# Two layers of attention and routed experts on one core: the queue that the maxima's rows are sent on, and when and how many blank rows are laid

## The chip, the cores and the metric

The kernel runs on one core of a Trainium2 chip. The time is what the device takes for one execution, in microseconds (us). It was measured in nine runs before the change, with a median of 740.36 us (735.84 to 743.92). One further execution was recorded by the hardware profiler. That one took 738.56 us, and all durations below are from it.

The core has five engines that each work through their own instructions in order: PE (TensorE, matrix products), DVE (VectorE), ACT (ScalarE), POOL (GpSimd) and SP (SyncE, which does nothing but issue transfers, load registers and wait). Transfers between DRAM and on-chip memory (DMA) are issued by SP, ACT or POOL, and carried out by 16 DMA engines. The profile names the queue of a transfer: q1 holds what SP issues, q10 what ACT issues, q0 what POOL issues.

## The reference

Four steps, each added to `x` (8 blocks of 256 tokens, 128 wide, 2048 tokens in all):

```python
x = x + _L0_xattn_ref(_layernorm(x), ctx, ctx, mask, mask, Wq, bq, Wk, bk, Wv, bv)
x = x + _L0_ffn_ref(_layernorm(x), W_router, b_router, W1, b1, W2, b2)
x = x + _L1_xattn_ref(_layernorm(x), ctx, ctx, w_q, w_k, w_v, w_o)
x = x + _L1_ffn_ref(_layernorm(x), W_gate, Wg, Wu, Wd)
```

Layer 0's attention has 16 heads of width 8, and a pair of tokens whose mask bits differ gets -1e9 added to its score before the softmax. Layer 0's feed-forward part sends each token to the two of 8 experts with the largest logits, weighted with a softmax over these two:

```python
logits = flat_x @ W_router + b_router
top_vals, top_idx = jax.lax.top_k(logits, 2)
router_weights = softmax(logits, all but the two largest at -inf)
for e in range(8):
    h = relu(flat_x @ W1[e] + b1[e])          # 128 -> 512
    y = h @ W2[e] + b2[e]                     # 512 -> 128
    out = out + y * router_weights[:, e] * (token has e among its two)
```

Layer 1 is of the same kind: causal attention with 16 heads of width 64 and an output projection, and experts of width 352 with a silu gate.

## The kernel before

**Layer 0's attention.** One step of the main loop (its counter `n`) handles a pair of heads of one tile of queries. For block `b`, `scores` computes the scores q k for 125 of 128 contraction rows and DVE takes each query's maximum (L546, L550). The softmax needs that maximum subtracted. It is subtracted by the matrix product itself: rows 125 to 127 of the query operand `q9` hold the maxima, split in three bf16 parts, and the same rows of the key operand `k9` hold -1. `probs` then computes the transposed scores anew with all 128 rows (L577), and ACT takes the exponential (L584). `probs` runs `LAG` = 15 steps behind `scores`.

The rows of maxima come from `maxima(b, hf)`, once for each half of the heads, so 16 times in all: DVE splits the maxima, PE transposes them (L565), ACT copies the result to `mT` (24 partitions of 256 bf16 values, L569), and a DMA of 12 KB sends `mT` into the three rows of `q9` (L570). SP issues that DMA. The first `probs` of the half wait for it.

SP also loads the operands of the blocks to come. In `prep0(b)`, which starts two blocks ahead, it sends four mask rows (L446), writes the three parts of q and k to DRAM in another layout (`rows<-part`, L531, six DMAs of 192 KB) and loads `q9` and `k9` from there (`q<-rows`, `k<-rows`, L534 and L535, 576 KB each). The parts are computed by POOL (L514 to L517). SP works in program order, so one of its instructions that waits holds all that come behind it.

**Routing.** `route` takes 4 (or 2) tiles of 128 tokens, finds each token's two experts and the slot in each expert's list, and POOL writes the token's normalised row there with an indirect DMA (`xs<-rows,ati`, L712: one DMA for 128 tokens and one of their two experts). `taken[l][:, k, e]` is the first free slot of expert `e` after `k` token tiles. Layer 0's first 12 of 16 token tiles (`NEARLY`) are routed while the attention runs, the last four after it.

Each expert's list is worked on in tiles of 128 rows, so rows that are no token's follow behind the last slot. They must hold a valid row address and a weight of zero, and are called blank rows. `blank` is a DRAM buffer of such rows, and `spread` copies from it into a stretch of an expert's list in `xs`. For layer 0 that is `tails(0)`: for each of the 8 experts SP loads the first free slot into a register (`values_load`) and issues a DMA there. Before the change this happens as soon as the first 12 token tiles are counted, with `taken` at tile 12, and each stretch is five tiles of 128 rows (640 rows of 520 bytes, 325 KB), so that it reaches past what the last four token tiles can add; their rows are written over it afterwards. Layer 1 lays its blank rows in another way (`blanks(1)`).

**Tables and experts.** `place(l, early)` makes the list of expert tiles. Its early call takes the 16 tiles that are full after 12 token tiles; its late call takes the other 23. `tab` holds the expert and the row of each tile. The expert loop `run` then works through the 39 tiles, four ahead with its loads: `look_up(j)` loads expert and row of tile `j` from `tab` into SP's registers, `fetch(j)` issues two DMAs, the tile's rows (`xj<-xs`, L815, 65 KB) and its expert's weights (`wj<-wa`, L822, 258 KB in layer 0 and 352 KB in layer 1), `flip` transposes the rows (`px`, L827, PE), `hidden` makes the hidden layer (`ph`, L842), and `result` the output, which POOL writes to `ys` with another indirect DMA (L882). The rows of an early tile wait only for the early scatters; those of a late tile wait for all scatters and for the blank rows.

**What sets the order.** PE, ACT, DVE and SP execute their instructions in the order in which the program text emits them. POOL's queue is left to a scheduler. Pieces of work that run beside the main loop are generators in the list `side`; each call of `tick()` advances each of them to its next `yield`. `one_by_one` puts generators behind one another in one of these. The end of the passage from attention to experts reads, in the main loop and behind it:

```python
        if n == NS * B + LAG - 2:
            begin0(range(4))
            tiles0 = run0()
        if n >= NS * B + LAG:
            next(tiles0)
    one_by_one(route(0, NT - QT, QT))
    one_by_one(place(0, False))
```

The first expert tiles are thus worked on while the last two token tiles are still being routed.

Of the kernel before, what the change touches and what calls it, by code (L numbers as in the profile page):

```python
# [17 lines left out]
P = 128  # L18
# [11 lines left out]
GT = G // P  # L30
NG = B * S // G
T = B * S
NT = T // P
# [3 lines left out]
NX = E * XT + E * P  # L37
# [4 lines left out]
NEARLY = NT - 4  # L42
EARLY = (16, 17)
FIRST = EARLY[0] + QT * E
HH = H // 2
# [8 lines left out]
R_ALL = P  # L54
R_MAX = R_ALL - NPART
# [7 lines left out]
def kernel(  # L63
# [28 lines left out]
    nc = tc.nc  # L92
# [7 lines left out]
    ET = mybir.EngineType  # L100
# [4 lines left out]
    def bank(tag, name, dt=F32):  # L105

        if tag == "any":
            third.append(third.pop(0))
            tag = third[-1]
        return ps.tile([P, 512 * 4 // mybir.dt.size(dt)], dt, tag=tag, name=name, bufs=1 if tag in ("pv", "y") else 2)  # L110

    writes = {}
    known = {}

    def after(dma, key, n=None):

        if n is not None:
            for group in (key + "late", key + "blank"):
                tc.declare_no_dep(dma.ins, group=group, reason="disjoint rows")
        tc.add_to_no_dep_group(key + "read", dma.ins)  # L120
        for w in writes.get(key, ())[:n]:
            tc.add_manual_dep(
                dma.ins, w.ins.name,
                mybir.DependencyInfo(mybir.DependencyClass.Sync, mybir.DependencyReason.DATA),
                reason="rows by index",
            )
        return dma
# [13 lines left out]
    side = []  # L141
# [46 lines left out]
    with nc.allow_non_contiguous_dma(reason="two rows of biases, once"):  # L188
        for i, src in enumerate((bq0, bk0)):
            nc.scalar.dma_start(  # L190
                out=brow[:, i, :].rearrange("o (d g j) -> o d g j", d=DK0, g=4),
                in_=src.rearrange("(o j z) g -> o z g j", o=1, z=32)[:, :DK0],
# [94 lines left out]
    q9s, k9s = [], []  # L287
# [23 lines left out]
    xs = [dr.tile([NX, ROW], F32, tag=f"xs{l}", name=f"xs{l}") for l in range(2)]  # L311
# [21 lines left out]
    taken = [cst.tile([P, NT + 1, E], F32, tag=f"tk{l}", name=f"tk{l}") for l in range(2)]  # L333
# [218 lines left out]
    def maxima(b, hf):  # L552

        mx = c0[b]["mx"][:, :, ts(hf, HH)]
        m3 = sm.tile([P, QT, NPART, HH], BF16, tag="m3", name=f"m3_{b}_{hf}")
        rest = sm.tile([P, QT, HH], F32, tag="mrest", name=f"mrest{b}_{hf}")
        nc.vector.tensor_copy(m3[:, :, 0, :], mx)
        nc.vector.tensor_tensor(rest, mx, m3[:, :, 0, :], ALU.subtract)
        nc.vector.tensor_copy(m3[:, :, 1, :], rest)
        nc.vector.tensor_tensor(m3[:, :, 2, :], rest, m3[:, :, 1, :], ALU.subtract)  # L560
        yield
        yield
        pm = bank("pt", f"pm{b}_{hf}", BF16)
        for qt in range(QT):
            nc.tensor.transpose(  # L565
                pm[: NPART * HH, ts(qt, P)], m3[:, qt].rearrange("p r h -> p (r h)"), ident_b
            )
        mT = sm.tile([NPART * HH, S], BF16, tag="mT", name=f"mT{b}_{hf}")
        nc.scalar.copy(mT, pm[: NPART * HH, :S])  # L569
        nc.sync.dma_start(out=q9s[b % 3][R_MAX:R_ALL, ts(hf, HH), :], in_=mT)  # L570
        yield

    def probs(b, h):
# [44 lines left out]
    def route(l, t0, GT, eng=nc.vector):  # L618
# [11 lines left out]
        def s8(tag):  # L630
            return sm.tile([P, GT, E], F32, tag=tag + str(GT), name=f"{tag}{name}", bufs=1)
# [48 lines left out]
        for i in range(GT):  # L680
            k = t0 + i
            eng.tensor_tensor(taken[l][:, k + 1, :], taken[l][:, k, :], pr[:, 1, i, :], ALU.add)
        if t0 + GT == NEARLY and l == 0:
            side.append(tails(l))
        rank = s8("rank")
        eng.tensor_tensor(rank, pr[:, 0], taken[l][:, tiles, :], ALU.add)
        slot = sm.tile([P, 2, GT, E], F32, tag=f"slot{GT}", name=f"slot{name}", bufs=1)
# [17 lines left out]
        for i in range(GT):  # L705
            for k in range(2):
                if eng is nc.gpsimd and (k == 0 or t0 < NEARLY - GT):
# [5 lines left out]
                        out=xs[l][:, :], out_offset=to, in_=rows[:, i, k, :], in_offset=None  # L713
# [5 lines left out]
    def place(l, early):  # L719

        n, m = (NEARLY, EARLY[l]) if early else (NT, NJ - EARLY[l])
        if early:
            known[f"xs{l}"] = len(writes[f"xs{l}"])
        name = f"{l}_{n}"
        cnt = sm.tile([P, E + 1], F32, tag="cnt", name=f"cnt{name}", bufs=1)
        nc.vector.tensor_tensor(cnt[:, :E], own, taken[l][:, n, :], ALU.mult)
        nc.vector.tensor_reduce(cnt[:, E:], cnt[:, :E], AX.X, ALU.add)
        cnt = cnt[:, E:]
        is_in = sm.tile([P, 2], F32, tag="isin", name=f"isin{name}", bufs=1)
        if early:  # L730
            nc.vector.tensor_scalar(is_in[:, 0:1], cnt, -float(P), what[:, 1:2], ALU.add, ALU.is_ge)
        else:
            nc.vector.tensor_tensor(is_in[:, 1:2], cnt, what[:, 1:2], ALU.is_gt)
            nc.vector.tensor_tensor(is_in[:, 0:1], is_in[:, 1:2], tabs[l, "taken"], ALU.subtract)
        in_b = sm.tile([P, 1], BF16, tag="inb", name=f"inb{name}", bufs=1)
        nc.vector.tensor_copy(in_b, is_in[:, 0:1])
        yield
        yield
        pos = bank("pt", f"pos{name}")[:, 0:1]
        nc.tensor.matmul(pos, lhsT=upper, rhs=in_b, start=True, stop=True)  # L740
        at = sm.tile([P, 1], F32, tag="pos", name=f"at{name}", bufs=1)
        nc.vector.tensor_copy(at, pos)
        pick = sm.tile([P, NJ], F32, tag="pick", name=f"pick{name}", bufs=1)
        nc.vector.tensor_scalar(pick[:, :m], order[:, :m], at, is_in[:, 0:1], ALU.is_equal, ALU.mult)
        if early:
            got = tabs[l, "taken"] = sm.tile([P, 1], F32, tag="got", name=f"got{name}", bufs=1)
            nc.vector.tensor_scalar(got, at, m - 0.5, is_in[:, 0:1], ALU.is_lt, ALU.mult)
        yield
        yield
        po = bank("pt", f"pick{name}")[:m, :3]  # L750
        nc.tensor.matmul(po, lhsT=pick[:, :m], rhs=what, start=True, stop=True)
        tab = sm.tile([P, 2], I32, tag=f"tab{early}", name=f"tab{name}", bufs=1)
        if early:
            nc.vector.tensor_copy(tab[:m, :], po[:, :2])
        else:
            sp = sm.tile([P, 4], F32, tag="sp", name=f"sp{name}", bufs=1)
            nc.vector.tensor_copy(sp[:m, :3], po)
            nc.vector.tensor_scalar(sp[:m, 3:4], sp[:m, 2:3], spare[:m, 1:2], spare[:m, 0:1], ALU.mult, ALU.add)
            nc.vector.tensor_copy(tab[:m, 0:1], sp[:m, 0:1])
            nc.vector.tensor_tensor(tab[:m, 1:2], sp[:m, 1:2], sp[:m, 3:4], ALU.add)  # L760
        tabs[l, early] = tab
        yield

    def spread(to, i):

        to = to.rearrange("(c a r) w -> a c (r w)", a=16, r=P // 16)
        src = blank[i, :, : P // 16 * ROW].unsqueeze(1)
        return nc.sync.dma_start(out=to, in_=src.to_broadcast(list(to.shape)))

    def tails(l):  # L770

        last = sm.tile([P, E], I32, tag="last", name=f"last{l}", bufs=1)
        nc.vector.tensor_copy(last, taken[l][:, NEARLY, :])
        m = NT - NEARLY + 1
        for i in range(E):
            if i % 2 == 0:
                yield
            row = nc.values_load(
                last[0:1, i : i + 1], engines=(ET.SP,), min_val=0, max_val=NX - m * P,
                skip_runtime_bounds_check_because="an expert has XT rows",  # L780
            )
            dma = spread(xs[l][bass.ds(row, m * P), :], i)

            for group in (f"xs{l}", f"xs{l}blank"):
                tc.declare_no_dep(dma.ins, group=group, reason="disjoint rows")
            tc.add_to_no_dep_group(f"xs{l}blank", dma.ins)
# [7 lines left out]
    def experts(l):  # L794
# [16 lines left out]
        def fetch(j):  # L811
            e, row, _ = regs[j]
            xj = wk.tile([P, ROW], F32, tag="xj", name=f"xj{l}_{j}", bufs=10)
            after(
                nc.sync.dma_start(out=xj, in_=xs[l][bass.ds(row, P), :]), f"xs{l}",  # L815
                known[f"xs{l}"] if j < EARLY[l] else None,
            )
            src = (wa0, wa1)[l]
            if j % 2 == 0:
                tiles["w"] = wk.tile([P, 2, 2 * FF1], F32, tag="pr", name=f"wj{l}_{j}", bufs=3)  # L820
            wj = tiles["w"][:, j % 2, : src.shape[2]]
            nc.sync.dma_start(out=wj, in_=src[bass.ds(e, 1), :, :].rearrange("o p w -> p (o w)"))  # L822
            tiles[j] = {"x": xj, "w": wj}

        def flip(j):
# [246 lines left out]
    def attention1(begin):  # L1072
        n = B * NU
        when = ((3, 3, 3, 3), (1, 1, 2, 3), (0, 1, 2, 3))
        for k in range(n + 4):
# [9 lines left out]
            if 0 <= bo < B and wo in (0, 1):  # L1085
                output(bo, wo)
                if wo == 1 and bo + 1 < B:
                    one_by_one(route(1, QT * bo, QT))
                    if QT * (bo + 1) == NEARLY:
                        one_by_one(place(1, True))  # L1090
# [51 lines left out]
    for n in range(NS * B + LAG + 3):  # L1142
        b, i = divmod(n, NS)
# [122 lines left out]
```

## Time and profile before

| | |
|---|---|
| median of nine runs | 740.36 us (735.84 to 743.92) |
| profiled execution | 738.56 us |
| its span, first to last instruction | 736.9 us |
| mean granted clock of PE | 0.941 |
| PE busy | 614.9 us (83%) |
| DVE busy | 483.0 us (66%) |
| POOL busy | 335.0 us (45%) |
| ACT busy | 331.9 us (45%) |
| DMA | 90.24 MB, 122 GB/s in the mean |
| `q<-mT`, SP | 16 DMAs of 12 KB |
| `xs<-blank` of layer 0's tails, SP | 8 DMAs of 325 KB |
| `xj<-xs`, `wj<-wa`, SP | 78 of each |
| `xs<-rows,ati`, POOL | 64 indirect DMAs, 987 ns each |

Layer 0's last probabilities are computed at 231 us, and its experts run from there to 341 us; layer 1's attention takes until 624 us, and its experts until 720. A line of a timeline gives the start, the duration, the engine, the line of the code, the operation, the tile that is written and those that are read, and how often; in brackets stands how long the engine was idle before it, and what ended that. A line of the waits gives the engine and its line, what it waited for, the total in us, how many times, and the longest. SPq is SP's issuing of a DMA, not the transfer itself.

### The profile page before, as it was taken

The numbers are of one execution on the slowest core, as the hardware profiler recorded it, in microseconds if no ns is written. First come the engines' busy times: TensorE is split into PE (matmuls) and PEld (weight loads), VectorE is DVE, ScalarE is ACT, GpSimd is POOL, SyncE is SP. The second block draws the span as 40 slices with busy tenths as digits, with TensorE's granted clock in tenths as the row PEclk, the third lists the DMA queues.
The fourth block names the chain that finished last, engine by engine and source line by source line (L and its number), as shares of the span: only waits on it lengthen the run. The fifth ranks groups of instructions, "written<-read, shape, count | busy, mean of one in ns | idle before, by whom it ended". The sixth has DMA issues, their size and how long they took to land.

```text
span 736.9 us, 15214 instructions
## 1 busy us (share of the span) xinstructions
PE 614.9 (83%) x4781; PEld 477.4 (65%) x4781; DVE 483.0 (66%) x1810; ACT 331.9 (45%) x1028; POOL 335.0 (45%) x401
## 2 busy tenths in 40 slices
PE   3488887587848689999999999999999887979990
PEld 2254454353525679997677777777777665869990
DVE  6876687575825465564867778787886875544453
ACT  1044555354532222324675665666665652423330
POOL 5554458434060444444433345445353643554443
PEclk9688999788988899999999999999999999999996
DMA  5566678544044456654873020000000004557755
GB/s 141 135 178 177 199 192 219 145 128 128 2 138 119 132 138 175 189 162 101 258 271 94 24 78 23 15 16 17 1 16 1 15 13 146 153 156 230 236 174 160
DMA packets 74030, 90.24 MB, mean 122 GB/s; under 512 B 9944, under 2 KB 55280, under 8 KB 72944
## 3 DMA queue, kind: packets, MB, share of 16 engines
q1 hardware_dynamic: 62952, 68.92, 33.3%
q0 software_dynamic: 7840, 18.97, 8.4%
q10 hardware_dynamic: 3160, 1.39, 0.8%
q8 instruction: 39, 0.64, 0.4%
q14 instruction: 39, 0.32, 0.2%
HBM read 67.25 MB, written 36.99 MB: 141 GB/s over the span
## 4 chain that ended last, share of the span: by engine, by line
PE 33%; DVE 11%; ACT 4%; DMA 3%; issue 2%; POOL 1%; ACTq 0%; SPq 0%; POOLq 0%; DVEq 0%
PE s L990 5%; PE y L1065 4%; PE y L875 3%; PE ph L852 3%; PE pt L1039 3%; PE o L1054 3%; PE pu L855 3%; DVE ns L1005 3%; PE pk L953 3%; ACT p L1016 2%; PE pq L953 2%; DMA yy<-ys 2%; DVE pT L1041 2%; DVE k L956 2%; PE pv L946 1%
## 5 line engine op out<-in xcount | busy, mean ns | idle before, releaser
L1016 ACT ACTIVATE p<-ns,nm 128x256 f32<-128x256 f32 (+1 forms) x256 | 113.8, 447 | 33.0 <-DVE nm L1005 28.8
L1029 POOL TENSOR_TENSOR p<-p,rd 128x1024 f32<-128x1024 f32 (+1 forms) x63 | 92.2, 1483 | 62.4 <-DVE rd L1024 60.0
L882 POOL DMA_INDIRECT ys<-yj,xj x78 | 75.3, 966 | 88.1 <-DVE yj L880 72.3
L584 ACT ACTIVATE pT<-st 128x512 f32<-128x512 f32 x128 | 73.8, 596 | 67.9 <-PE st L577 61.6
L550 DVE TENSOR_REDUCE mx<-sc 128x2 f32<-128x512 f32 x128 | 83.2, 683 | 30.5 <-PE sc L546 26.5
L712 POOL DMA_INDIRECT xs<-rows,ati x64 | 63.2, 987 | 79.7 <-DVE rows L704 52.8
L1005 DVE CUSTOM_DVE_ANT_0 ns<-s,tri 128x256 f32<-128x256 f32 (+1 forms) x256 | 77.0, 349 | 0.5 <-PE s L990 0.5
L577 PE MATMUL st<-q,k 128*128 128x256 bf16 x256 | 53.5, 294 | 20.6 <-DMA q<-mT 15.1
L546 PE MATMUL sc<-k,q 125*128 125x256 bf16 x256 | 54.5, 300 | 16.1 <-DVE mx L550 14.0
L1041 ACT COPY pT<-pt 128x512 f32<-128x512 f32 x64 | 36.8, 575 | 69.1 <-PE pt L1039 69.1
L1039 PEld LDWEIGHTS pt<-ident,p 128*128 128x128 f32 x384 | 45.2, 141 | 23.6 <-DVE k L956 11.0
L1039 PE MATMUL pt<-ident,p 128*128 128x128 f32 x384 | 56.8, 276 | 4.5 <-POOL p L1029 3.3
L1054 PE MATMUL o<-pT,v 128*64 128x256 f32 (+1 forms) x512 | 54.3, 334 | 4.9 <-ACT pT L1041 3.3
L845 ACT ACTIVATE h<-ph,wj 128x128 f32<-128x128 f32 x78 | 24.4, 364 | 67.1 <-issue 49.5
L990 PE MATMUL s<-k,q 64*128 64x256 f32 (+1 forms) x512 | 53.2, 338 | 0.5 <-DVE nm L1005 0.5
L842 PE MATMUL ph<-xT,wj 128*128 128x128 f32 x312 | 46.7, 295 | 7.8 <-DVE xT L829 5.5
L861 DVE TENSOR_TENSOR h<-s,pu 128x256 f32<-128x256 f32 x78 | 24.0, 349 | 40.5 <-PE px L827 20.2
L1054 PEld LDWEIGHTS o<-pT,v 128*64 128x64 f32 x512 | 35.0, 136 | 23.6 <-issue 6.2
L990 PEld LDWEIGHTS s<-k,q 64*128 64x128 f32 x512 | 42.8, 186 | 10.3 <-issue 4.5
L546 PEld LDWEIGHTS <-q 125*128 125x128 bf16 x256 | 24.0, 104 | 38.3 <-issue 33.7
L1016 ACT ACTIVATION_READ_ACCUMULATOR p<-ns,nm 128x1 f32 x256 | 48.6, 190 | 0.0
L842 PEld LDWEIGHTS ph<-xT,wj 128*128 128x128 f32 x312 | 40.3, 201 | 10.3 <-DVE xT L829 6.3
(231 smaller groups left out, 1287.6 us busy)
## 6 DMA issues: line engine op xcount, KB each, us to landing
wj<-wa SPq DMA_DIRECT2D x39, 352.0 KB
wj<-wa SPq DMA_DIRECT2D x39, 258.0 KB
xs<-blank SPq DMA_DIRECT2D x8, 1105.0 KB
rows<-part SPq DMA_DIRECT2D x42, 192.0 KB
xj<-xs SPq DMA_DIRECT2D x78, 65.0 KB
q<-rows SPq DMA_DIRECT2D x7, 576.0 KB
k<-rows SPq DMA_DIRECT2D x7, 576.0 KB
yy<-ys SPq DMA_DIRECT2D x13, 256.0 KB
```

The lines of the kernel that those rows point to most:

```text
L546: nc.tensor.matmul(sc[:, k, :], lhsT=q9s[b % 3][:R_MAX, h, ts(qt, P)], rhs=k9s[b % 3][:R_MAX, h, :], start=True, stop=True,)
L550: pace[0] = nc.vector.tensor_reduce(c0[b]["mx"][:, qt, 2 * u : 2 * u + 2], sc, AX.X, ALU.max)
L584: nc.scalar.activation(pT.rearrange("p t s -> p (t s)"), st, AF.Exp)
L712: nc.gpsimd.indirect_dma_start(out=xs[l][:, :], out_offset=to, in_=rows[:, i, k, :], in_offset=None),
L842: nc.tensor.matmul(phs[z][:, ts(i, P)], lhsT=wj[:, o : o + P], rhs=xT, start=True, stop=True)
L882: free(f"ys{l}", nc.gpsimd.indirect_dma_start(out=ys[l][:, :], out_offset=to, in_=yj, in_offset=None))
L990: nc.tensor.matmul(u["s"][a, r][:, (1 - qt) * S : (1 - qt) * S + n], lhsT=c1[b]["q"][rows, c, ts(qt, P)], rhs=c1[b]["k"][rows, c, :n], sta ...
L1005: nc.vector.tensor_tensor_reduce(out=ns[:, o : o + n], in0=s[:, o : o + n], in1=tri[:, S - n :], scale=-1.0, scalar=3.0e38, op0=ALU.add, o ...
L1016: nc.scalar.activation(p[:, o : o + n], ns[:, o : o + n], AF.Exp, bias=nm[:, a : a + 1], scale=-1.0, accum_out=u["sum"][:, 2 * i + a : 2 * ...
L1029: eng.tensor_tensor(p, p, rd[:, :, a : a + 1].to_broadcast([P, 4, n]), ALU.mult)
L1039: nc.tensor.transpose(pt[:, ts(n, P)], u["p"][:, i, (S, 0, P)[m] :][:, :P], ident)
L1054: nc.tensor.matmul(o[DK1 * r : DK1 * (r + 1), a, t * P :], lhsT=v[:, t, cols], rhs=pT, start=(t == 0), stop=True, skip_group_check=True,)
```

## The change

There are three edits. The DMA from `mT` to `q9` is issued by ACT in place of SP. `tails(0)` no longer starts in `route` after 12 token tiles; the late call of `place` runs it, with the slots after all 16 token tiles, and one tile of 128 rows (65 KB) for each expert instead of five. Its parts are interleaved with that of `place`: the cast of the slots to integers (`last`) follows the cast `in_b`, three of the blank DMAs come at the next tick and the other five at the one after. And `fetch` issues the weights of a tile ahead of its rows, in both layers. In SP's order the eight blank DMAs, each with its register load, stand between the fetch of layer 0's tile 12 and the look-up and fetch of tile 13.

```diff
-        nc.sync.dma_start(out=q9s[b % 3][R_MAX:R_ALL, ts(hf, HH), :], in_=mT)
+        nc.scalar.dma_start(out=q9s[b % 3][R_MAX:R_ALL, ts(hf, HH), :], in_=mT)
...
-        if t0 + GT == NEARLY and l == 0:
-            side.append(tails(l))
...
         nc.vector.tensor_copy(in_b, is_in[:, 0:1])
-        yield
-        yield
+        fills = iter(()) if early or l == 1 else tails(l)
+        next(fills, None)
+        yield
+        next(fills, None)
+        yield
+        next(fills, None)
         pos = bank("pt", f"pos{name}")[:, 0:1]
...
             nc.vector.tensor_scalar(got, at, m - 0.5, is_in[:, 0:1], ALU.is_lt, ALU.mult)
+        for _ in fills:
+            pass
         yield
...
         last = sm.tile([P, E], I32, tag="last", name=f"last{l}", bufs=1)
-        nc.vector.tensor_copy(last, taken[l][:, NEARLY, :])
-        m = NT - NEARLY + 1
+        nc.vector.tensor_copy(last, taken[l][:, NT, :])
         for i in range(E):
-            if i % 2 == 0:
+            if i % 3 == 0:
                 yield
             row = nc.values_load(
-                last[0:1, i : i + 1], engines=(ET.SP,), min_val=0, max_val=NX - m * P,
+                last[0:1, i : i + 1], engines=(ET.SP,), min_val=0, max_val=NX - P,
                 skip_runtime_bounds_check_because="an expert has XT rows",
             )
-            dma = spread(xs[l][bass.ds(row, m * P), :], i)
+            dma = spread(xs[l][bass.ds(row, P), :], i)
...
             xj = wk.tile([P, ROW], F32, tag="xj", name=f"xj{l}_{j}", bufs=10)
-            after(
-                nc.sync.dma_start(out=xj, in_=xs[l][bass.ds(row, P), :]), f"xs{l}",
-                known[f"xs{l}"] if j < EARLY[l] else None,
-            )
...
             nc.sync.dma_start(out=wj, in_=src[bass.ds(e, 1), :, :].rearrange("o p w -> p (o w)"))
+            after(
+                nc.sync.dma_start(out=xj, in_=xs[l][bass.ds(row, P), :]), f"xs{l}",
+                known[f"xs{l}"] if j < EARLY[l] else None,
+            )
```

## The prediction

> **What bounds the kernel now.** I read the slices of the page first, then the waits of TensorE (PE) in the stage of layer 0's attention, then the timeline and the short windows around the one stretch where PE stands still longest, and last the loads of the expert tiles. Each digit below is the busy tenths of PE in a slice of 18.4 us.
>
> ```profile
> PE   3488887587848689999999999999999887979990
> ```
>
> From slice 15 on (276 us) PE is busy nine tenths and more: nothing that the change touches there can give much. The loose time lies before 280 us, in layer 0's attention (20 to 205 us, PE busy 139.5 of 185) and in the passage to the experts (200 to 280 us). Who PE waits for from 20 to 205 us (total, times, longest):
>
> ```profile
> PE sc L546 <- DVE mx L550: 14.0, 15, 4.8
> PE st L577 <- DMA q<-mT: 15.1, 5, 7.1
> PE st L577 <- DMA k<-mrow: 2.7, 1, 2.7
> PE st L577 <- ACT pT L584: 1.4, 4, 0.7
> ```
>
> DVE's maxima pace the stage, but 15.1 us go to the row of maxima (mT) that is sent into q9. The 2.7 under k<-mrow is also such a wait: it precedes the first probabilities of block 2 and ends when mT has landed. ScalarE (ACT) holds PE for only 1.4 us. One of these sends (us from the start; duration; in brackets the idle time before):
>
> ```profile
> 57.45 0.80 SPq L570 DMA_DIRECT2D q<-mT  x1
> ...
> 63.67 0.58 PE L577 MATMUL st<-q,k 128*128 128x256 bf16 x2 [3.08 <-DMA q<-mT]
> ...
> 134.62 1.03 SPq L278 DMA_DIRECT2D xs<-blank  x2
> ...
> 143.02 0.80 SPq L570 DMA_DIRECT2D q<-mT  x1
> ...
> 145.35 0.61 PE L577 MATMUL st<-q,k 128*128 128x256 bf16 x2 [7.14 <-DMA q<-mT]
> ```
>
> Two kinds of lateness: at 57 us SP issues at once, but the 12 KB land 6 us later, since packets of the preceding q<-rows and k<-rows loads (8192 B each, on the same queue, from 53.0 to 62.8 us) go first. In the second, mT was copied by 135.6 us, but SP issued it at 143.02, behind blank rows that waited for POOL, mask rows and rows<-part.
>
> The passage:
>
> ```profile
> 209.91 12.19 SPq L768 DMA_DIRECT2D xs<-blank  x8
> ...
> 218.04 0.96 POOL L712 DMA_INDIRECT xs<-rows,ati  x1 [0.31 <-issue]
> 221.34 0.59 ACT L600 COPY oT<-o 128x512 f32<-128x512 f32 x1 [5.41 <-remote]
> 221.98 1.11 PE L605 MATMUL po<-ident,oT 128*128 128x128 f32 x4 [7.01 <-ACT oT L600]
> ```
>
> ```profile
> 216.00:218.00 2.00, 0.00 (x0) 0.00 (x0) 0.00 (x0) 0.00 (x0) 1.43 (x2) 1.00 0.84 241
> ...
> 222.00:224.00 2.00, 2.00 (x6) 1.37 (x7) 1.57 (x8) 0.42 (x1) 0.89 (x2) 0.50 0.72 223
> ```
>
> (Columns: length, then PE, weight load, DVE, ACT, POOL busy, granted clock, DMA share, GB/s.) While POOL issues eight scatters in a row and 2.66 MB of blank rows fill the DMA engines, PE, DVE and ACT do nothing for 7 us; ACT's copy waits for a matmul that had started by 213.7. Afterwards the clock stands at 0.50 until 226, and at 0.86 for two more.
>
> **Part 1, mT on ACT's queue.** It takes 16 issues of 0.70 to 0.82 us off SP and puts them into ACT's order. PE's waits for mT, by first probabilities: 1.38 (51.8 us), 3.08 (63.7), 2.69 (85.1), 0.60 (106.6), 2.90 (129.6), 7.14 (145.4), in all 17.8. The first four, 7.75, fall away if mT no longer queues behind the row loads (uncontended, its packets come some 1.4 us after the issue). The last two, 10.0, do not go whole: the next block's rows hang on POOL's work from 116 to 134.6 us, then SP's to 150.1, landing 158.6; PE would only wait there instead. I count 3.25. So 11 is saved.
>
> Against it: 16 x 0.75 = 12 us more of ACT's order, with the next exponentials (0.60 each) behind each issue, and PE's second matmul after them. ACT is busy 85.0 of 185 us there and sits 55.9 us in front of exponentials for PE, so most is hidden by PE's own pace; if that cover were gone it would cost 12. I take 3.5, a quarter of an issue and more each time. SP, freed, sends rows<-part of blocks 3, 4, 5 and 7 some 2 to 6 us earlier, so these loads are not late next. The issues do not wait on ACT for long: the transfer whose semaphore each one reuses was issued 12 us or more before. Part 1: 11 - 3.5 = 7.5, bounds +17.8 and -12.
>
> The Trainium skill ("DMA: Bandwidth & Descriptors", "Issuing engines are not separate DMA queues") speaks against this part: transfers started by ScalarE or SyncE share the same 16 engines, and issuing from two only saves sequencer time. By that rule only the 7.4 us that SP kept mT back would go, and by the cap above no more than 3.25 of them, so part 1 would be about nothing; the trace's packets, in order on one queue, are why I side with the larger sum, and no run here yet shows mT on the other queue.
>
> **Part 2, the blank rows.** Removed at 209.9: eight issues, 12.19 us of SP, 8 x 325 KB. What they cost is the stillness (7.0 us) and the slow clock after it (4 us at 0.50 and 2 at 0.86, 2.3 lost): 9.3 if they alone make it; nothing if the scatters do. Rows between: eight scatters in a row from 166.3, with 1.15 MB of row loads at a DMA share of 0.52, came with a PE gap of 3.73 us (170.3 to 174.0); four scatters and two of ys at 242 to 249.6, with shares of 0.11 to 0.29, with 4.66. Both have far less traffic than 0.84 to 0.90, and both leave a gap: I let 2.8 of the 9.3 stay, and count 6.5 (bounds 0 and 9.3). SP's earlier tab loads and first fetches hide behind PE: the first tile is wanted at 234.07, 7.5 us after its rows landed.
>
> Added: `last` cast after the late table's input (DVE, 0.15 us), and eight issues of 65 KB between the fetch of tile 12 and that of 13. Behind them on SP stand the look-up and fetch of 13, then PE.
>
> ```profile
> 264.13 0.33 SPq L815 DMA_DIRECT2D xj<-xs  x1
> ...
> 278.60 0.27 PE L827 MATMUL px<-ident,xj 128*128 128x128 f32 x1
> ```
>
> This is tile 13 now: rows landed at 266.4, 12.2 us ahead of use. After, `last` is there at about 267.7 (DVE's inb at 267.44). One blank costs SP between 1.1 us (a 65 KB blank transfer at 142 us took 1.17 for two, 0.58 each, plus a register load and address arithmetic of about half a microsecond) and 1.52 (12.19/8 now). Eight: 8.8 to 12.2, to 276.5 to 279.9. Then look-up 0.65, wj 0.55, and xj's landing 2.4: 280.1 to 283.5, against 278.6. PE stalls 1.5 to 4.9; I take 3. Bounds 0 (it falls into the gap at 272 that exists anyway) and 6 (plus that gap growing by the blanks' 0.53 MB). After it SP needs 1.25 us a tile and PE 2.12, so the lead recovers. Part 2: 6.5 - 3 = 3.5.
>
> **Part 3, wj before xj in 78 fetches.** Same issues, other order. xj comes at most 2 us later; in both layers it lands 5.3 us or more before use in the steady stretch. Nothing, with that lead as the cover; without it up to 0.5 a tile.
>
> **Sum**: 738.56 (the profiled execution; span 736.9) - 7.5 - 3.5 = 727.6. The median shown is 1.8 above that execution, so 729.4; I say 729.
>
> **Rivals.** (A) The scatters' burst alone makes the stillness: it stays, the blanks give 0 and cost 3. For: the gaps at 170 and 246 us without blanks. Against: 7 us here is the longest, at the highest DMA share. 740.4 - 7.5 + 3 = 735.9. (B) mT was covered anyway: PE, released earlier, meets DVE's maxima or the next rows. For: POOL's chain before block 6, and 14.0 us of waits for maxima already. Against: four of the six waits have no such neighbour. 740.4 - 0 - 3.5 = 736.9; with A, 743.4 at worst, some 740 in the middle. (C) Slower: the eight late blanks starve PE at tile 13. The stall is 267.75 + 8p + 3.6 - 278.6 = 8p - 7.25 for p us a blank; it decides from p = 2.66, where it eats 7.5 + 6.5. At p = 3.2 it is 18.4: 744.8. For: in the present row of L768 single issues reach 7.2 us and register moves 0.87, and four scatters run at that moment. Against: a fifth of the bytes, and half of the issues take 0.60 or less. (D) Better: the stillness goes whole, stall covered: 740.4 - 11 - 9.3 = 720.1.
>
> **How the numbers follow.** Forecast 0.45, D 0.15, A 0.15, B 0.08, A and B together 0.06, C 0.11. A measurement of this kernel tells about 0.5%, 3.7 us, from no change: faster means below 736.7. Forecast and D are faster, two thirds of A and of B too: 0.75. The rest of A and B, and both together: 0.14. C: 0.11. The range reaches from a little below D to A with B: 717 to 740.
>
> **What would show it.** Part 1: waits for q<-mT below 5 us, ACT's pT waits of PE up by no more than 4, first probabilities of blocks 1, 2 and 3 no later than 2.5 us after mT's copy. Part 2: SP without L768 at 210 us, PE's gap there 4 us or less; eight blank issues after `last`, 9 to 12 us, and a PE wait for xj or wj of 1.5 to 5 us at tile 13, none at tile 17. Part 3: no wait of px or ph for a DMA later. Wrong would be: an unchanged 7 us gap at 215 (A), waits for DVE or k<-rows that grow by what mT's lose (B), over 14 us before tile 13 (C).

## The result, and the profile after

| | before | after |
|---|---|---|
| median | 738.91 us (62 runs) | 759.69 us (20 runs) |
| ratio, 95% interval | | 1.0276 (1.0253 to 1.0299) |
| profiled execution, span | 736.9 us | 757.8 us |

The change makes the kernel 2.8% slower, some 20 us. Forecast were 729 us and faster, in a range of 717 to 740.

The slices of PE in the profile after (18.9 us each) show where: the fourth and the ninth, 57 to 76 and 152 to 171 us, stood at 8 before and are at 4 now, and the sixteenth (284 to 303 us) fell from 9 to 7.

```profile
PE   3494887646877687999899999999999887979991
```

(The digits before stand with the prediction.) The first scores of block 2 come 6.2 us later than before, those of block 6 12.9 and those of block 7 15.1 later. The first expert tile is 12.1 late, tile 16 15.8. The rest of the 20.9 comes after that, in layer 1. Whom PE waits for from 20 to 225 us in the profile after (total, times, longest):

```profile
PE sc L546 <- DMA k<-rows: 23.0, 2, 11.9
PE sc L546 <- DVE mx L550: 15.8, 18, 4.8
PE st L577 <- DMA q<-mT: 9.2, 5, 3.2
```

The waits for mT did shrink, from 17.8 to 9.2. But there is a new one, 23.0 us for the loads of k9, which the profile before did not have. What SP waited for in that stretch tells why:

```profile
SPq L531 <- DMA q<-mT: 13.4, 3, 6.5
SPq L535 <- DMA rows<-part: 9.9, 7, 3.2
SPq L340 <- DMA q<-mT: 8.7, 1, 8.7
...
SPq L282 <- DMA q<-mT: 5.0, 1, 5.0
```

SP no longer issues mT, and yet it waits for mT: with its rows<-part (L531), its k<-minus (L340) and its blank<-blank (L282), none of which reads or writes mT. The loads of k9 before, for blocks 2 and 6:

```profile
54.16 0.30 SPq L535 DMA_DIRECT2D k<-rows  x1
...
150.10 0.31 SPq L535 DMA_DIRECT2D k<-rows  x1
```

The timeline of these two stretches after:

```profile
50.47 9.72 SPq L531 DMA_DIRECT2D rows<-part  x6
...
55.73 0.72 ACTq L570 DMA_DIRECT2D q<-mT  x1
...
61.24 0.32 SPq L534 DMA_DIRECT2D q<-rows  x1
63.46 0.31 SPq L535 DMA_DIRECT2D k<-rows  x1
...
70.30 0.59 PE L546 MATMUL sc<-k,q 125*128 125x256 bf16 x2 [11.13 <-DMA k<-rows]
...
152.33 6.03 SPq L282 DMA_DIRECT2D blank<-blank  x2
...
155.63 0.72 ACTq L570 DMA_DIRECT2D q<-mT  x1
...
163.86 0.32 SPq L535 DMA_DIRECT2D k<-rows  x1
...
172.46 0.58 PE L546 MATMUL sc<-k,q 125*128 125x256 bf16 x2 [11.90 <-DMA k<-rows]
```

The six rows<-part of block 2, 0.6 us each, stretch over 9.7 us, because the third of them stands until the mT that ACT issues at 55.73 has landed. The load of k9 goes out at 63.46, where it was 54.16 before, and PE stands for 11.13 us. Before block 6 the same happens with two blank<-blank rows (152.33, 6.03 us for two); the load of k9 goes out at 163.86 against 150.10, and PE stands for 11.90 us.

The reason stands in the program as it is built, in which every transfer names the semaphore that it adds to and the count that its issue waits for. A transfer announces its landing on a completion semaphore. SP and ACT share eight of these, dealt out in turn, in the order in which the scheduler expects the issues; in this program a transfer isn't issued until the one before it on its semaphore has landed. As long as SP issues mT, that predecessor is older in SP's own order. With mT on ACT the deal runs over two engines, and the scheduler expected ACT to be ahead of SP. The predecessors of the two transfers that hold the loads up longest:

```
transfer on SP                  before                      after
rows<-part, block 2, third      k<-minus (SP)               mT of block 1, first half (ACT)
blank<-blank, fourth            k<-mrow of block 6 (SP)     mT of block 5, first half (ACT)
```

One more of SP's transfers got an mT as its predecessor early on: a k<-minus follows the first mT, and stands 8.7 us for it (L340 above), before the loads of block 2.

The passage to the experts, before (the gap at the last scatters) and after:

```profile
273.97 1.76 PE L842 MATMUL ph<-xT,wj 128*128 128x128 f32 x8 [2.30 <-DVE h L846]
```

```profile
274.31 0.33 SPq L823 DMA_DIRECT2D xj<-xs  x1
279.35 11.10 SPq L772 DMA_DIRECT2D xs<-blank  x8
...
288.03 2.08 PE L845 MATMUL ph<-xT,wj 128*128 128x128 f32 x8 [5.54 <-DVE sp L761]
...
291.34 0.33 SPq L823 DMA_DIRECT2D xj<-xs  x1
...
293.88 0.33 PE L830 MATMUL px<-ident,xj 128*128 128x128 f32 x1 [1.26 <-DMA xj<-xs]
```

The eight late blank rows take SP 11.1 us (8.8 to 12.2 were forecast), tile 13's rows go out 17 us after tile 12's, and PE waits 1.26 us for them. Ahead of that lies a gap of 5.54 us at the last scatters; at its place before the gap had 2.30. The gap at the eight scatters shrank from 7.01 to 2.92.

### The profile page after: what moved, and what is told of

Its sections match the earlier page's. It is cut to its first block, busy times and chain, and to the rows that moved or that the text cites. A ratio compares the mean times of both kernels' runs of the same rounds, so it can differ in the third digit from the quotient of the medians.

```text
span 757.8 us, 15198 instructions
## 1 busy us (share of the span) xinstructions
PE 617.9 (82%) x4781; PEld 478.9 (63%) x4781; DVE 486.0 (64%) x1810; ACT 332.5 (44%) x1028; POOL 335.1 (44%) x401
## 4 chain that ended last, share of the span: by engine, by line
PE 33%; DVE 10%; ACT 5%; DMA 2%; issue 2%; POOL 1%; ACTq 0%; POOLq 0%
PE s L993 5%; PE y L1068 4%; PE y L878 4%; PE pt L1042 3%; PE o L1057 3%; PE ph L855 3%; PE pu L858 3%; ACT p L1019 3%; PE pk L956 3%; DVE ns L1008 2%; PE pq L956 2%; DVE k L959 2%; DMA yy<-ys 2%; DVE pT L1044 2%; PE pv L949 1%
```

## The experiments

They ran in three batches, each with the kernel before on the same chip. Its median was 716.9 us in the first two and 741.1 in the third: chips differ by 3%, so times are compared within a batch, and traces with care.

**1. mT on ACT alone.** The kernel before with

```diff
-        nc.sync.dma_start(out=q9s[b % 3][R_MAX:R_ALL, ts(hf, HH), :], in_=mT)
+        nc.scalar.dma_start(out=q9s[b % 3][R_MAX:R_ALL, ts(hf, HH), :], in_=mT)
```

> The kernel before, with only the sends of mT moved to ACT's queue. Theory S (shared completion semaphores: SP and ACT deal out eight of them in the scheduled order, so SP transfers of the loads of blocks 2 and 6 wait until an mT that ACT sends later has landed): slower by 14 to 18 us, with two PE waits of 11 to 12 us for k<-rows, before the scores of blocks 2 and 6. Rival L (the late blank rows and the order of the fetches make the loss): within 4 us of before, no PE wait for k<-rows.

Measured: 737.4 against 716.9 us, 1.0267 (1.0211 to 1.0323). PE's longest waits, from 20 to 205 us:

```profile
PE st L577 <- DMA q<-mT: 14.6, 6, 4.2
PE sc L546 <- DVE mx L550: 13.3, 18, 4.3
PE sc L546 <- DMA k<-mrow: 12.9, 1, 12.9
PE sc L546 <- DMA k<-rows: 12.3, 1, 12.3
```

One line makes a loss as large as that of the whole change, 20.5 us where 14 to 18 were expected, with two waits of over 12 us (the first ends before block 2's scores, though the view names mask rows). SP waited for mT with the same three lines as in the kernel after.

**2. The kernel after with mT back on SP** (the line of experiment 1 reversed).

> The kernel after, with the sends of mT back on SP's queue; the late blank rows and weights-first fetches stay. Theory S: within 5 us of before, no PE wait for k<-rows above 2 us; about 4 us are gained at the eight scatters (gap of 7.0 down to 3) and given back at tile 13 (a gap of 5.5 instead of 2.3 while the blank rows are laid, and 1.3 for the rows). Rival L: slower than before by 14 us or more.

Measured: 722.1 against 716.9 us, 1.0078 (1.0043 to 1.0112). That is 5.2 us slower, just outside the 5 that theory S allowed; PE's wait for k<-rows is 1.6 us. Rival L falls. On this chip PE's wait for xj at tile 13 is 5.7 us.

**3. Weights ahead of rows alone.** The kernel before with the two DMAs of `fetch` exchanged, as in the change.

> The kernel before, with only the order of the two transfers in fetch changed (weights, then rows). Theory S: no change, within 2 us, since rows landed 5 us ahead of use. Rival W (the order costs in layer 1, whose profiled part from its first scores to the end is 5.1 us longer in the kernel after): slower by 4 to 5 us, nearly all after 341 us.

Measured: 720.6 against 716.9 us, 1.0044 (1.0013 to 1.0075). The interval is 0.9 to 5.4 us. A difference of zero lies outside it, but both the 2 us that theory S allowed and the 4 to 5 of rival W lie within, so it doesn't decide between them.

**4. mT on ACT, moved in the deal of semaphores.** The kernel before with

```diff
-        nc.sync.dma_start(out=q9s[b % 3][R_MAX:R_ALL, ts(hf, HH), :], in_=mT)
+        dma = nc.scalar.dma_start(out=q9s[b % 3][R_MAX:R_ALL, ts(hf, HH), :], in_=mT)
+        if sent:
+            behind(dma, sent[-4 if hf else -1])
...
-                nc.sync.dma_start(out=to[i], in_=part[:, :, n, :])
+                sent.append(nc.sync.dma_start(out=to[i], in_=part[:, :, n, :]))
```

> The kernel before with mT on ACT's queue, each send also made to wait for an SP transfer of the same or the next block's parts (rows<-part) that is issued well before it. That moves the sends behind these transfers in the scheduled order, so the semaphores of the loads of block 2 and of the blank<-blank rows before block 6 are no longer those of a later mT. Theory S: the PE waits for k<-rows fall below 3 us, those for mT stay below 7 in all, and the time is 4 to 10 us less than before. Rival Q (ACT's queue itself is the cost: issues in front of the exponentials, packets): slower than before by 10 us or more, as with mT on ACT alone.

Measured: 724.7 against 716.9 us, 1.0115 (1.0083 to 1.0147). The waits for k<-rows are gone, and with them 12.7 of the 20.5 us that experiment 1 lost on this chip. In the built program the two transfers of the table follow SP's own transfers again. SP still waits for mT elsewhere, 38.2 us in eight waits of at most 7.4, and PE has no wait for k<-rows from it. But the kernel isn't faster than before, and the waits for mT did not fall:

```profile
PE st L580 <- DMA q<-mT: 15.3, 7, 3.7
...
PE st L580 <- DMA rows<-part: 5.1, 1, 5.1
```

The 5.1 us, and 3.7 of the 15.3, stand at the two sends that the added dependence held back, by 2.05 and 1.73 us after mT's copy. The other sends went out within 0.03 us of their copies, and PE still waited 11.6 us for them. So theory S is right on what makes the two long waits and wrong on what would be left without them: a queue of its own does not bring mT forward beside the loads. Where the 7.8 us that this kernel still loses lie was not settled.

**5. The kernels before and after once more, on one chip.**

> The kernel before, unchanged, for its trace on the chip that the other kernels of this batch run on. If the long gaps of PE at POOL's scatters (3.7, 7.0, 4.7 and 2.3 us in the first trace) belong to the code, they are here again; if they belong to that chip or that execution, the span is 15 to 25 us shorter and most of them are missing, as in the traces of the kernels with mT on ACT alone and with weights first alone.

> The kernel after, unchanged, on the same chip as the kernel before. Slower by 18 to 23 us; two PE waits of 11 to 13 us before the scores of blocks 2 and 6, and a wait of PE for xj at tile 13 of 4 to 6 us if the scatter gap is missing there (it hides the blank rows otherwise).

After: 739.7 against 716.9 us, 1.0309 (1.0269 to 1.0348). The unchanged kernel before has no gap of 7 us at the eight scatters here. What it has at that place is this:

```profile
213.03 0.96 POOL L712 DMA_INDIRECT xs<-rows,ati  x1 [0.30 <-issue]
...
219.93 0.19 POOL L624 COPY rows<-dest 128x4 int32<-128x4 int32 x1 [5.94 <-DMA xs<-rows,ati]
...
220.84 0.74 DVE L414 TENSOR_SCALAR rows<-x,mvr,rsr 128x256 f32<-128x256 f32 x2 [4.42 <-POOL rsr L403]
...
222.24 0.69 PE L422 MATMUL npr<-ident,rows 128*128 128x128 f32 x2 [4.38 <-DVE v L947]
```

Read from the end: PE waits for DVE, whose copy v (L947) stands behind the normalised rows of token tiles 12 and 13; DVE waits for POOL, and POOL's copy into the buffer of rows for the scatters of tiles 8 to 11, which still read a buffer that it takes. They land beside 2.66 MB of blank rows. With the late blank rows the same copy waited 2.24 us (experiment 6). In the traces of the two faster batches PE's wait here is 2.5 to 5.1 us with the early blank rows (experiments 1, 3, 4 and the kernel before) and 0 to 2.3 with the late ones (2, 6 and the kernel after), so this is most likely what the early ones cost. In experiment 7 a late mT covers it.

The kernel after, on the same chip, from 20 to 345 us:

```profile
PE sc L546 <- DMA rows<-part: 12.9, 1, 12.9
PE sc L546 <- DMA k<-rows: 12.1, 1, 12.1
PE px L830 <- DMA xj<-xs: 5.6, 1, 5.6
```

**6. The late blank rows almost alone.** The kernel after with mT back on SP and, in layer 1, the rows ahead of the weights again. Layer 0 keeps the weights first.

> The kernel after with mT back on SP, and with the weights ahead of the rows in layer 0 only (there the late blank rows need it, since the program does not let the blank rows follow directly on a load of rows in SP's order). This leaves the late blank rows alone. Theory B (late blanks cost one stall of 4 to 6 us at tile 13 and give back what the early ones took): +1 to +4 us. Rival W (the order in layer 1 made the 5 us of the kernel with mT back): no slower than before, while that kernel is 0.8% slower.

Measured: 721.4 against 716.9 us, 1.0063 (1.0040 to 1.0086). Against the trace of the kernel before on this chip, the last scores of layer 0 come 1.6 us earlier, the first tile 6.4, tile 12 8.0, and tile 16 0.2 later: 6.4 us won between the scores and tile 12, where the scatters land earlier, and more than that given back from tile 13 on (PE waits 5.6 us for its rows). The loss of 4.5 us, slightly more than theory B's 1 to 4, is not in these two executions: they took 719.0 and 719.8 us. Rival W's condition, no slower than before, isn't met. Its interval and that of experiment 2 overlap, so the order in layer 1 stays open.

**7. mT on POOL's queue**, `nc.gpsimd.dma_start` in the line of experiment 1, in the kernel before.

> The kernel before with mT sent by POOL, whose transfers have completion semaphores of their own. Theory S (semaphores shared by ACT and SP make the loss): no PE wait for k<-rows above 3 us, although SP has as little to do as with ACT; the time within 6 us of before, with waits for mT of 10 to 20 us in all where POOL is at its own work. Rival F (any send off SP's queue disturbs the loads, since SP runs ahead and the loads collide): waits of about 12 us for k<-rows again, and 15 us or more slower.

Measured: 731.5 against 716.9 us, 1.0207 (1.0174 to 1.0240). The scores of blocks 2, 3 and 4 come +0.6, -1.3 and -2.5 us against before, no wait for k<-rows of 12 us appears, and SP waits for mT nowhere. Rival F falls. The kernel is 14.6 us slower, where theory S expected at most 6, and the waits for mT are longer. The longest, 11.1 us, has two parts: POOL sends that mT 6.2 us after its copy (114.44 against 108.28 us), and packets of row loads run until 121.29.

```profile
PE st L577 <- DMA q<-mT: 22.5, 9, 11.1
...
PE sc L546 <- DMA rows<-part: 4.1, 1, 4.1
```

**8. Two of the sixteen sends back on SP**, in the kernel before with mT on ACT:

```diff
+        queue = nc.scalar if (b, hf) not in ((1, 0), (5, 0)) else nc.sync
+        queue.dma_start(out=q9s[b % 3][R_MAX:R_ALL, ts(hf, HH), :], in_=mT)
```

> The kernel before with mT on ACT's queue, but for two of the sixteen: the first halves of blocks 1 and 5 stay on SP. Theory S (in the deal of semaphores these two are the ones that hold up the loads of blocks 2 and 6): both PE waits of 12 to 13 us for loaded rows fall below 4 us, and 10 us or more of the 20 that mT on ACT costs are gone. Rival Q (each send on ACT costs something, in proportion): still 16 to 19 us slower than before.

Measured: 745.0 against 741.1 us, 1.0063 (1.0027 to 1.0100). From 20 to 205 us:

```profile
PE st L578 <- DMA q<-mT: 19.8, 6, 6.7
...
PE sc L546 <- DMA k<-rows: 1.1, 1, 1.1
```

Two sends out of sixteen carry three quarters of the loss (1.0267 in experiment 1, on another chip, down to 1.0063), as theory S says, and both long waits are gone. In the built program the two transfers of the table follow SP's own again. Of the 19.8 us, 12.4 stand at the two sends on SP.

The 4 us that are left arise ahead of block 2's scores. These come 3.7 us later than in experiment 9, on the same chip (67.27 against 63.55 us), and layer 0's last scores still only 3.5. SP's k<-minus stands 9.4 us for the first mT here, which fits; a kernel without that wait was not run. From block 2 on, in these two traces, the sends on ACT neither win nor lose.

**9. A buffer of its own for the rows of token tiles 12 and 13**, in the kernel before: `route(0, 12)` writes into the space of `q9s[2]`.

> The kernel before, in which the routing of token tiles 12 and 13 writes its rows into a buffer that no scatter still reads (the space of q9 of block 5, no longer used). Theory L (what the early blank rows cost is not PE's stillness as such: their 2.66 MB make the eight scatters land late, and POOL's copy into the rows' buffer, which the scatters still read, holds that routing and PE): PE's wait before the rows' transposes, 4.4 us in the trace of the unchanged kernel on the faster chip, falls below 1, and the time by 2 to 5 us. Rival D (the blanks' traffic delays whatever comes next): the wait only moves, to the first tile's rows, and the time is within 1 us.

Measured: 741.5 against 741.1 us, 1.0021 (0.9986 to 1.0056). PE does not wait before the rows' transposes, but nor does the kernel before in the first trace: this batch's chip has the long gaps again, and PE stands a little earlier for the other reason:

```profile
220.96 2.05 PE L957 MATMUL pk<-c,wk 128*128 128x256 f32 x4 [4.63 <-DVE on L610]
```

So it can't be said here what the buffer brings where that gap is missing. The 2 to 5 us of theory L did not come.

**10. As experiment 9, and one mT on ACT**, that of block 4's second half.

> As the kernel with a buffer of its own for the rows of token tiles 12 and 13, and a single mT on ACT's queue: that of the second half of block 4, which SP holds back for 7 us behind the blank rows that wait for POOL. By what follows it in the deal of semaphores only blank<-blank rows wait for it, at a time when it has landed. Theory S: 1 to 4 us less than with the buffer alone (the wait of 5 us falls to 2, part of it comes back before block 6). Rival C (the loads of block 6, which hang on POOL, take all of it): within 1 us of it.

Measured: 740.2 against 741.1 us, 1.0013 (0.9972 to 1.0053). Against experiment 9 that is 1.3 us less, which the intervals do not tell from nothing or from 4, so the times decide neither theory S nor rival C. The trace sides with C: the wait for that mT falls from 5.90 (experiment 9) to 1.89 us, and the next one, at the first probabilities of block 5, grows from 1.03 to 4.65.

**11. The late blank rows spread**: two ahead of the fetch of tile 13, two ahead of 14, four ahead of 15, in the kernel of experiment 2.

> The kernel after with mT back on SP, and the eight late blank DMAs spread out in SP's order: two ahead of the fetch of tile 13, two ahead of 14, four ahead of 15. Theory P (the stall at tile 13 is SP's time for eight blanks, 1.4 us each, ahead of that fetch): no wait at tiles 13 and 14, 2 to 3 us at tile 15 or 16, and 2 to 4 us less than the kernel with mT back alone, so within 0.5% of before. Rival T (their traffic or their landing makes the stall): 5 us or more at tile 16, no gain.

Measured: 746.2 against 741.1 us, 1.0051 (1.0013 to 1.0090). No wait at tiles 13 and 14, as theory P has it, but 4.8 us at tile 15 where it expected 2 to 3 (in a profiled execution of 749.4 us, longer than the median). So little or nothing is won against experiment 2's 1.0078, on another chip; spreading moved the stall.

No version beat the kernel before.

## Why the prediction was wrong, point by point

**Part 1, the semaphores: wrong, and this is the step that failed.** The prediction said of the sends on ACT that "the transfer whose semaphore each one reuses was issued 12 us or more before". ACT indeed never stands for it: in the trace after each of the 16 goes out 0.03 us after its copy. But the prediction asked the question for the engine that got the transfers and not for the one that lost them: SP's older transfers now reuse the semaphores of ACT's younger ones. From "SP, freed, sends rows<-part of blocks 3, 4, 5 and 7 some 2 to 6 us earlier" it concluded that "these loads are not late next". The rows<-part of these blocks went out 4.2 to 12.0 us later in the trace after (block 3 at 66.68 against 62.53), and the loads of blocks 2 and 6 cost PE 23.0 us. The term stood at 7.5 us of gain (bounds +17.8 and -12) and is a loss of 20.5 us on the chip of experiment 1, outside both. Experiments 1, 4, 7 and 8 show it: the one line makes the loss, and the two long waits go when the order of the deal, the set of semaphores, or two of the sends change. What 4, 7 and 8 still lose was explained only in part.

The 3.5 us charged for ACT's issues did not show in PE's waits for exponentials: 1.1 us in the trace after, against 1.4.

**Part 1, the queue: wrong.** "The first four, 7.75, fall away if mT no longer queues behind the row loads", the prediction said. The trace after has an mT on a queue of its own beside such loads, and it waits for them all the same:

```profile
76.81 0.75 ACTq L570 DMA_DIRECT2D q<-mT  x1
...
82.95 0.61 PE L577 MATMUL st<-q,k 128*128 128x256 bf16 x2 [3.25 <-DMA q<-mT]
```

Its packets, on q10, start at 81.59 us and end at 82.34. Between its issue and that start, 94 packets of 8192 B of the row loads start on q1, the first at 76.82, and the last ends at 81.74. Where no loads run, mT's packets start 1.4 us after the issue (55.73 and 57.10). Of the 9.2 us left of the 17.8, 6.2 stand beside row loads (3.25 here, 2.93 at block 4), and 2.9 beside rows<-part and blank rows. Of the waits that went, two went where the loads were late: the mT at 55.73 found the DMA engines free because SP stood. In experiment 4, with the loads nearly in time, PE's waits for mT were back at 15.3.

One of the first four never belonged to this group. The mT behind the wait of 1.38 us at 51.8 was issued at 48.17, before the packets of the row loads (from 53.0); SP had kept it 1.5 us behind rows<-part. On ACT it went out at once, and that wait is gone.

The Trainium skill ("DMA: Bandwidth & Descriptors", "Issuing engines are not separate DMA queues") had said so: transfers from several engines share the same 16 DMA engines, and only the time to issue is saved. The prediction had weighed this and sided with the trace's packets, which could not tell one queue's order from the engines' load. Here the rule agrees with the runs.

**Part 1, the gain kept for blocks 5 and 6 (3.25 us): too much.** Experiment 10 sends early the mT that SP had held back, and of the 4.0 us won there 3.6 come back at the next half, whose mT stands beside the loads of block 6.

**Part 2, the blank rows removed: the size about right, the reason wrong.** The prediction took 6.5 of the 9.3 us of stillness and slow clock as the blank rows' price. In experiment 5 that stillness does not exist in the same code. There the price seems to be the wait of POOL's copy for the scatters, and with the late blank rows (experiment 6) the first tile comes 4.8 us earlier after the last scores; from the first trace to the trace after it comes 4.2 earlier. The line was there in the trace before, 3.31 us of POOL's idle time ahead of L624 ended by a scatter, but the prediction did not look at it. Where the gaps exist, this one was 7.0 and 6.5 us with the early blank rows (the first trace and experiment 8), 4.6 and 3.6 with them and the buffer of its own (experiments 9 and 10), and 4.3 and 2.9 with the late ones (experiment 11 and the kernel after). Some 3 to 4 us stay without the early blank rows; that these lengthen the gap is likely from the first two figures, but the others overlap, and it is not shown.

**Part 2, the stall at tile 13: right in place and kind, too small.** Forecast were 3 us (1.5 to 4.9, with bounds of 0 and 6) from 8 blanks of 1.1 to 1.5 us. SP's time was within that (8.8 to 11.1 us for eight), and the stall is 5.6 to 5.7 us on the faster chips. What was off is the moment at which PE wants tile 13: the gap at the last scatters that gives SP time is missing there. On the slower chip, where it exists, it grew from 2.30 to 5.54, and 1.26 are left for tile 13: 4.5 in sum.

**Part 3: nothing was forecast**, and experiment 3 says 0.44% (0.13 to 0.75). Where that lies was not found.

**The rivals.** The price of C, "the eight late blanks starve PE at tile 13", was worked out rightly from the first trace (8p - 7.25 with p of 1.1 to 1.4 is 1.6 to 4.0), against 4.5 to 5.7 measured, and it decides nothing alone. Rival B had the right outcome for the one mT of experiment 10, a wait that comes back elsewhere, but no loss. None had the right slower case, since all looked at what stands behind the moved instruction, and none at who reuses its semaphore.

## What to carry to other kernels

Before a DMA is moved to another engine's queue, look in the built program at both sides of its completion semaphore: whom it waits for, and which later transfers will wait for it. If the engine that gets it runs ahead of the other in the scheduler's order, old transfers end up waiting for young ones. And here a second queue did not lift a small transfer past large ones that the DMA engines were already working on.

## What was not expected of the hardware

The same kernel took 717 us on some chips and 739 to 741 on others. The traces of the slower ones show gaps at POOL's bursts of indirect DMAs, during which PE, DVE and ACT all stand (3.7, 7.0, 4.7 and 2.3 us in the first trace, with a clock of 0.50 for some 4 us after the longest); those of the faster ones show none of this kind there (the 4.38 us of PE in experiment 5 come from POOL's copy). A gap seen in one profile is thus not yet a property of the code. What makes the gaps was not found.
